# Layer 1's product with the eigenvector matrix as a burst on 64x64 blocks, and a second rank for the last units

## The chip, the cores and the metric

The kernel runs on one core of a Trainium2 chip. The time is the device time of one launch in microseconds, from the first to the last instruction of the program with what lies around it; less is better. Everything is fp32.

## The reference

Four graph layers follow each other on x, 128 graphs of 64 nodes with 256 features. Each is added to its input and normalised: `x = layernorm(x + layer(x))`.

- Layer 0: three times `(adj * adj) @ (h @ W)`, with relu after the first two; widths 512, 1024, 256.
- Layer 1: U holds the eigenvectors of a Laplacian of adj (found on the core itself). `agg = U.T @ x`, `h = relu(agg @ W1 + b1)` with 128 columns, `out = U @ (h @ W2 + b2)`.
- Layer 2: two graph convolutions with adj, then for p = 1 to 4 an LSTM over every window of p nodes (hidden size 256), whose last state replaces the window's last node.
- Layer 3: attention of each graph's nodes over each other, masked with adj.

## The kernel before, in words

The 8192 rows are cut into 16 groups of 512, that is 8 graphs. A tile of 128 rows holds two graphs, so a matrix over the nodes such as adj or U stands in a 128x128 tile with its 64x64 block twice on the diagonal (`adT2`, `adH2`, `u2`, `ut2`).

Until some 833 us layer 0 runs group by group, with the eigenvectors computed beside it. This stage is left as it was. From there on the 16 groups go through layers 1 to 3. Two groups form a unit, with its own instructions: `layer1` and `to_lstm` for each group (the latter with the steps for p = 1, `singles`, and p = 2, `pairs`), then `long` for p = 3 and p = 4 on both groups together, then `from_lstm` and `layer3` for each group. A step of an LSTM is `fast`: seven block products instead of eight for each gate, with sums and differences taken on DVE. Each step needs the state `hs` of the step before. The last unit is groups 14 and 15 (`ENDING`); its turns of data are done on PE, while the other groups' go through DVE transposes and a round trip through DRAM (`across`: one store and four loads on SP's queue). In `layer3` of the other groups there are two such round trips and eight small transfers of the attention weights.

In `layer1`, `mixed` applies U.T: 32 products on 64x64 blocks, four blocks of the array side by side, into two PSUM tiles that DVE and ACT copy out. Then comes the product with W1, bias and relu into `h`; then the turned product: with `h` as the held operand and `ut2` as the moving one, PE gives U applied to h, transposed, as `z`; then the product with W2. The turned product was made of 128x128 products, half of whose moving operand is zero, so four for each group.

The order of the instructions of all engines is written out by a planner, `Plan`. Every operation is noted with a cost and with what it depends on. `Plan.run` repeatedly picks the engine whose next operation can start first by its own clock, and on that engine, of the operations that can start within 0.02 us of the earliest, the one with the lowest `rank`. Up to four units (`UNITS`) are in progress; `todo` holds those that haven't begun. The rank is normally `op.due`, which is the group's number times `PERIOD` (17 us) less `op.tail`, the length of the chain of work that follows the operation. When nothing is left in `todo` and at most two groups (`LASTS`) are unfinished, PE prefers the group with more operations left. Buffers are slots by kind: eight PSUM tiles (`ps`), nine work tiles (`w`), four row tiles (`rows`) and so on. On the chip each engine then takes its instructions strictly in the order written, with semaphores for what comes from elsewhere; since they are emitted in one helper, nearly all of them have the line L162 in the profile.

Of the kernel before, what the change touches and what calls it, by code (L numbers as in the profile page):

```python
# [11 lines left out]
F32 = mybir.dt.float32  # L12
# [4 lines left out]
N = 64  # L17
# [86 lines left out]
class Plan:  # L104
# [59 lines left out]
    def run(self, units, ways):  # L164

        going, todo, held, left, wanted = {}, list(enumerate(units)), {}, {}, {}
        able = {e: [] for e in self.engines}

        def rank(op):
            if op.engine == "PE" and not todo and len(left) <= LASTS:  # L170
                return -left[op.group]
            return op.due

        def candidates(guard):
            oldest = min([u for u in going if u] or [0])
            best = None
            for e, ops in able.items():
                first = []
                for op in ops:
                    t = max(self.free[e], op.ready)  # L180
                    needs = {}
                    for tile in op.tiles:
                        if tile.real is None:
                            needs[tile.tag] = needs.get(tile.tag, 0) + 1
                    for tag, n in needs.items():
                        s = self.slots[tag]
                        t = max(t, sorted(s)[n - 1])

                        if (guard and op.unit != oldest and sum(x < 1e9 for x in s) < n +
                                min(self.MOST.get(tag, 1) - held.get((oldest, tag), 0), wanted.get((oldest, tag), 0))):  # L190
                            t = 1e9
                    if t < 1e9:
                        first.append((t, op))
                if first:
                    t0 = min(t for t, _ in first)
                    t, op = min((x for x in first if x[0] <= t0 + 0.02), key=lambda x: (rank(x[1]), x[1].rank))
                    if best is None or t < best[0]:
                        best = t, op
            return best

        while todo or going:
            while todo and len(going) < ways + (0 in going):
# [4 lines left out]
                for op in reversed(self.ops):  # L207
                    op.tail = op.cost + max([x.tail + (self.OWN if x.engine == op.engine else self.LAG)[op.engine]
                                             for x in op.after] or [0.0])
                    op.due = op.group * PERIOD - op.tail  # L210
                for tile in {tile: 0 for op in self.ops for tile in op.tiles if tile.real is None}:
# [5 lines left out]
            t, op = (candidates(True) if todo or len(left) > LASTS else None) or candidates(False)  # L217
            e = op.engine
            for tile in op.tiles:
                if tile.real is None:  # L220
                    s = self.slots[tile.tag]
# [533 lines left out]
P = 128  # L755
D = 256
# [8 lines left out]
OUTS = 2  # L765
LASTS = 2
PERIOD = 17.0
FARS = 8

RING = 4  # L770
QUADS = 1.17
# [58 lines left out]
def kernel(  # L830
# [25 lines left out]
    nc = tc.nc  # L856
    V, S, PE = nc.vector, nc.scalar, nc.tensor
# [5 lines left out]
    def tl(pool, shape, tag, **kw):  # L863
        uid[0] += 1
        return pool.tile(shape, F32, tag=tag, name=f"{tag}_{uid[0]}", **kw)
# [63 lines left out]
    ut2 = keep.tile([P, P], F32, name="ut2")  # L929
# [39 lines left out]
    def run(out, pairs):  # L969
        for i, (lhsT, rhs) in enumerate(pairs):  # L970
            mm(out, lhsT, rhs, i == 0, i == len(pairs) - 1)

    def relu(dst, src):
        S.activation(dst, src, AF.Relu)  # L974

    def quads(c):
        for m in (slice(0, N), slice(N, P)):
            for h, hs in enumerate((slice(0, N), slice(N, P))):
                yield m, slice(c * P + m.start, c * P + m.stop), h, hs
# [23 lines left out]
    spare = [lambda: tl(pa, [P, D], "spare")]  # L1003
    pending = []

    def step(then=None):

        while pending:
            pending.pop(0)()
        if then:  # L1010
            pending.append(then)
        if norms:
            norms.pop(0)()

    def bank(tag="ps"):
        return tl(psa, [P, 512], tag, bufs={"ps": 4, "ch": 2, "b5": 1}[tag])
# [40 lines left out]
    def seven(n, product, c11, c12, c21, c22, last):  # L1057

        def view(b):
            return b[:, :2 * n].rearrange("p (i n) -> p i n", i=2)  # L1060

        def add(dst, b):
            VL.tensor_add(dst, dst, b)
            if last is relu:
                relu(dst, dst)

        ch = view(bank("ch"))
        product(ch, 1, True)
        step(lambda: S.copy(c11, ch))
        yield  # L1070
        b2 = view(bank())
        product(b2, 2, True)
        step(lambda: add(c11, b2))
        yield
        product(ch, 6, False)
        step(lambda: S.copy(c12, ch))  # L1076
        yield
        b5 = view(bank("b5"))
        product(b5, 5, True)
        step(lambda: S.copy(c22, b5))  # L1080
        yield
        product(ch, 7, False)
        step(lambda: add(c22, ch))
        yield
        product(b5, 3, False)
        step(lambda: add(c12, b5))
        yield
        product(ch, 4, False)
        step(lambda: last(c21, ch))
        yield  # L1090
# [111 lines left out]
    wb = ctx.enter_context(tc.tile_pool(name="wb", bufs=1, reuse_waits="tile"))  # L1202
# [20 lines left out]

    far = [aside.tile([P, 1024], F32, name=f"far{i}") for i in range(FARS)]

    def place(tag, slot, shape):
# [8 lines left out]
        if tag in ("w", "v", "gates", "c", "hs"):  # L1235
# [3 lines left out]
    plan = Plan({"PE": nc.tensor, "DVE": nc.vector, "ACT": nc.scalar, "POOL": nc.gpsimd, "SP": nc.sync}, place,  # L1239
                {"ps": 8, "w": WIDE, "v": NARROW, "gates": GATES, "c": CELLS, "hs": OUTS, "att": ATT, "far": FARS, "rows": RING, "mx": 4, "sm": 4, "st": 4, "mv": 4,  # L1240
                 "rs": 4, "nm": 4})
    V, S, G, Q = (Noted(plan, e) for e in ("DVE", "ACT", "POOL", "SP"))
# [33 lines left out]
    def products(calls, also=(), **kw):  # L1276

        size = lambda x: x.at.size if isinstance(x, Part) else int(np.prod(x.shape[1:]))
        cost = sum(max(0.001673 * size(c[2]) + 0.003, 0.223) for c in calls)
        plan.note("PE", [("matmul", (o, l, r), {"start": a, "stop": z, **kw}) for o, l, r, a, z in calls], cost,  # L1280
                  also=also)
# [8 lines left out]
    def work():  # L1290
        return plan.tile("w", [P, 1024])

    def work2():
        return plan.tile("v", [P, 512])

    def ps4(shape=(P, 512)):
        return plan.tile("ps", shape)

    def as3(t, a):
        return t.rearrange("p (a b) -> p a b", a=a)  # L1300

    def relu(dst, src):
        S.activation(dst, src, AF.Relu)

    def mixed(src, rhs):

        dst = as3(work(), 2)
        to = dst.rearrange("p c (t h n) -> p h c t n", h=2, n=N)
        ps = [ps4((P, 2, 4, N)) for _ in range(2)]
        plan.note("PE", [("matmul", (ps[h][m, c, t, :], src[hs, t, f], rhs[hs, hs]), {"start": True, "stop": True})  # L1310
                         for t in range(4) for c in range(2) for m, f, h, hs in quads(c)], QUADS)
        V.tensor_copy(to[:, 0], ps[0])
        S.copy(to[:, 1], ps[1])
        return dst
# [22 lines left out]
    def layer1(xs):  # L1337
        a = mixed(xs, u2)
        for t in range(0, 4, 2):
            V.tensor_add(xs[:, t:t + 2, :], xs[:, t:t + 2, :], ub2.unsqueeze(1).to_broadcast([P, 2, D]))  # L1340
        h = as3(work2(), 4)
        z = work2()
        pz = ps4((P, 4, P))
        for t in range(0, 4, 2):
            p = ps4((P, 2, P))
            for j in range(2):
                run(p[:, j, :], [(a[:, k, (t + j) * P:(t + j + 1) * P], bw1[:, k, :]) for k in range(2)])
            V.tensor_add(h[:, t:t + 2, :], p, wide["b_b1"].unsqueeze(1).to_broadcast([P, 2, P]))
            relu(h[:, t:t + 2, :], h[:, t:t + 2, :])
            products([(pz[:, i, :], h[:, i, :], ut2, True, True) for i in (t, t + 1)])  # L1350
        S.copy(as3(z, 4), pz)
        for t in range(0, 4, 2):
            p = ps4((P, 2, D))
            for j in range(2):
                run(p[:, j, :], [(z[:, (t + j) * P:(t + j + 1) * P], bw2)])
            V.tensor_add(xs[:, t:t + 2, :], p, xs[:, t:t + 2, :])
            norm(xs[:, t:t + 2, :], False, twice=True)
# [388 lines left out]
```

## Time and profile before

| what | us |
|---|---|
| three runs | 2305.53, 2307.65, 2307.74 |
| median | 2307.65 |
| the profiled execution, own time | 2305.56 |
| its span from the first to the last instruction | 2303.8 |
| PE busy in the span | 2250.2 |
| weight loads busy (PEld) | 1985.7 |
| DVE busy | 1730.2 |
| ACT busy | 1196.0 |
| first instruction of layer 1 on PE | 832.8 |
| last product on PE starts | 2292.2 |

A row of the profile names the line, the engine, the operation, the tiles it writes and reads (out<-in, buffer numbers left out) and how many there are. PE is the matmul, PEld the weight load that runs beside it, DVE and ACT are the vector and the scalar engine, SP issues transfers. Matmuls are pipelined, so their durations overlap: the distance from one start to the next is what a product costs. An fp32 product appears as two records. In square brackets stands how long an engine was idle and which work ended that.

### The profile page before, as it was taken

To read this page: it belongs to the slowest core of one execution; us is meant where nothing else is said; L and a number is where in the kernel's file an instruction comes from. 1 tells how busy PE (TensorE), PEld (TensorE's weight loads), DVE (VectorE), ACT (ScalarE), POOL (GpSimd) and SP (SyncE) were. 2 spreads that over 40 slices of the span, in tenths; PEclk is the share of its full clock that TensorE was granted. 3 is DMA by queue.
4 is the path that set the end of the run, shared out by engine and by line. 5 is a ranking of instruction groups with operands and counts; after the bars stand their busy time and mean duration, and the time that the engine had idled before them with its cause. 6 is when DMAs were issued, how large, how long until landed. Compare 5 with 4: busy or idle time off the path is not lost.

```text
span 2303.8 us, 51099 instructions
## 1 busy us (share of the span) xinstructions
PE 2250.2 (98%) x20132; PEld 1985.7 (86%) x20132; DVE 1730.2 (75%) x5704; ACT 1196.0 (52%) x2892; POOL 137.0 (6%) x315
## 2 busy tenths in 40 slices
PE   8999999999999989999999999999999999999996
PEld 6788888878888778999989999899899899998895
DVE  5887877777888878666857967867866876878764
ACT  3444444443444336655556655555555655655654
POOL 0000000000000010000100100100000000000001
PEclk9999999999999999999999999999999999999998
DMA  7000000000000040000201211221211211312300
GB/s 242 11 11 11 10 11 11 19 11 11 11 10 2 1 161 20 19 1 27 85 22 57 75 56 40 78 72 40 77 56 49 76 65 31 104 58 93 99 19 19
DMA packets 80113, 107.87 MB, mean 47 GB/s; under 512 B 23296, under 2 KB 64256, under 8 KB 79872
## 3 DMA queue, kind: packets, MB, share of 16 engines
q1 hardware_dynamic: 79520, 104.32, 14.1%
q8 instruction: 158, 2.59, 0.5%
q14 instruction: 83, 0.68, 0.1%
q10 hardware_dynamic: 352, 0.28, 0.0%
HBM read 57.64 MB, written 45.09 MB: 45 GB/s over the span
## 4 chain that ended last, share of the span: by engine, by line
PE 86%; DVE 9%; ACT 1%; DMA 1%; issue 1%; POOL 1%; SPq 1%; DVEq 0%; ACTq 0%; POOLq 0%
PE ps L162 53%; PE ch L965 14%; PE ps L965 9%; PE b L965 6%; PE ps L1030 2%; DVE w L162 1%; DVE X L162 1%; DVE gates L162 1%; DVE st L162 1%; POOL rs L162 1%; DMA w<-far 1%; ACT gates L162 1%; PE pa L312 1%; SPq L162 1%; DVE D L52 1%
## 5 line engine op out<-in xcount | busy, mean ns | idle before, releaser
L162 PE MATMUL ps<-w,wih 128*128 128x128 f32 (+2 forms) x2944 | 573.0, 298 | 5.1 <-DVE gates L162 4.2
L162 PEld LDWEIGHTS ps<-w,wih 128*128 128x128 f32 x2944 | 454.3, 191 | 40.0 <-issue 13.5
L162 PE MATMUL ps<-w,sums 128*128 128x128 f32 (+2 forms) x3104 | 476.8, 294 | 5.7 <-DVE w L162 5.1
L162 PEld LDWEIGHTS ps<-w,sums 128*128 128x128 f32 x3104 | 419.9, 191 | 23.4 <-DVE w L162 6.4
L162 ACT ACTIVATE gates<-gates,cbi 128x256 f32<-128x256 f32 (+4 forms) x736 | 314.5, 479 | 189.0 <-DVE gates L162 186.0
L162 DVE TENSOR_TENSOR gates<-gates,ps 128x512 f32<-128x512 f32 (+4 forms) x408 | 235.9, 583 | 191.6 <-PE ps L162 182.4
L162 ACT COPY gates<-ps 128x512 f32<-128x512 f32 (+4 forms) x408 | 205.0, 507 | 238.1 <-PE ps L162 232.7
L162 PE MATMUL ps<-hs,whh 128*128 128x128 f32 (+1 forms) x896 | 182.2, 285 | 2.3 <-DVE hs L162 2.3
L162 PE MATMUL ps<-w,whh 128*128 128x128 f32 (+1 forms) x896 | 181.1, 284 | 0.0
L162 PEld LDWEIGHTS ps<-hs,whh 128*128 128x128 f32 x896 | 140.6, 193 | 2.5 <-DVE hs L162 2.5
L162 ACT ACTIVATE gates<-ps,cbi 128x128 f32<-128x128 f32 (+2 forms) x368 | 119.3, 385 | 42.2 <-PE ps L162 41.0
L162 PEld LDWEIGHTS ps<-w,whh 128*128 128x128 f32 x896 | 139.7, 191 | 0.0
L974 ACT ACTIVATE h<-h 128x512 f32<-128x512 f32 x96 | 60.5, 630 | 150.2 <-DVE h L52 150.2
L965 PE MATMUL ch<-m,tw 128*128 128x256 f32 x512 | 124.9, 382 | 3.0 <-ACT h L1076 1.7
L965 PE MATMUL b<-ss,aw 128*128 128x256 f32 x512 | 121.9, 379 | 0.0
L965 PE MATMUL ps<-aw,m 128*128 128x512 f32 x256 | 116.2, 606 | 1.2 <-ACT m L1036 1.2
L965 PEld LDWEIGHTS ch<-m,tw 128*128 128x128 f32 x512 | 94.7, 190 | 19.1 <-DVE h L52 3.7
L965 PEld LDWEIGHTS b<-ss,aw 128*128 128x128 f32 x512 | 96.8, 190 | 12.9
L162 POOL TENSOR_SCALAR rs<-mv 128x2 f32<-128x2 f32 x96 | 25.3, 272 | 1353.1 <-DVE mv L162 1351.7
L965 PEld LDWEIGHTS ps<-aw,m 128*128 128x128 f32 x256 | 48.3, 194 | 55.5 <-issue 51.5
L162 PE MATMUL ps<-hs,sums 128*128 128x128 f32 (+1 forms) x448 | 90.6, 284 | 0.0
L1036 ACT COPY m<-ps 128x512 f32<-128x512 f32 x96 | 51.2, 587 | 75.5 <-PE ps L1030 75.0
(360 smaller groups left out, 4077.4 us busy)
## 6 DMA issues: line engine op xcount, KB each, us to landing
far<-w SPq DMA_DIRECT2D x42, 512.0 KB, 2.7
w<-far SPq DMA_DIRECT2D x168, 128.0 KB, 3.2
X<-rest SPq DMA_DIRECT2D x24, 512.0 KB, 3.4
out_dram<-X SPq DMA_DIRECT2D x64, 128.0 KB, 1.7
rest<-XA SPq DMA_DIRECT2D x12, 512.0 KB, 2.6
rest<-X SPq DMA_DIRECT2D x12, 512.0 KB, 2.7
XA<-in_x_dram SPq DMA_DIRECT2D x22, 256.0 KB, 6.0
aw<-in_a_w_dram SPq DMA_DIRECT2D x3, 1024.0 KB, 10.2
```

Source lines behind the costliest of these rows:

```text
L52: return getattr(self.engine, name)(out, *args, **kw)
L162: getattr(e, name)(*[real(x) for x in args], **{k: real(v) for k, v in kw.items()})
L312: PE.matmul(out, lhsT, rhs, start=True, stop=True)
L965: PE.matmul(out, lhsT, rhs, start=start, stop=stop, **kw)
L974: S.activation(dst, src, AF.Relu)
L1030: PE.matmul(p[h][m, k, t, :], src[hs, t, f], sqT2[hs, hs], start=True, stop=True)
L1036: S.copy(to[:, h, c:c + 2], p[h])
```

## The change

Two things are changed in the program. In `layer1` the four turned products become one burst of 16 products on the four 64x64 blocks of the array; the halves of the result go to two PSUM tiles, of which DVE copies one and ACT the other. In `Plan.run` the rank of an operation is `op.due` only as long as some unit hasn't begun; from then on it is the group's number times `LATE` (8 us) less the tail. Also, the program is made with a smaller scratch for transfers that are described at run time (`dynamic_dma_scratch_size=1024`), and some helper functions are added that nothing calls.

```diff
         def rank(op):
             if op.engine == "PE" and not todo and len(left) <= LASTS:
                 return -left[op.group]
-            return op.due
+            return op.due if todo else op.group * LATE - op.tail
...
 PERIOD = 17.0
+LATE = 8.0
...
         h = as3(work2(), 4)
         z = work2()
-        pz = ps4((P, 4, P))
         for t in range(0, 4, 2):
             p = ps4((P, 2, P))
             for j in range(2):
                 run(p[:, j, :], [(a[:, k, (t + j) * P:(t + j + 1) * P], bw1[:, k, :]) for k in range(2)])
             V.tensor_add(h[:, t:t + 2, :], p, wide["b_b1"].unsqueeze(1).to_broadcast([P, 2, P]))
             relu(h[:, t:t + 2, :], h[:, t:t + 2, :])
-            products([(pz[:, i, :], h[:, i, :], ut2, True, True) for i in (t, t + 1)])
-        S.copy(as3(z, 4), pz)
+        pz = [ps4((P, 4, N)) for _ in range(2)]
+        plan.note("PE", [("matmul", (pz[b][m, i, :], h[bs, i, m], ut2[bs, bs]), {"start": True, "stop": True})
+                         for i in range(4) for m, _, b, bs in quads(0)], QUADS / 4 + 0.2)
+        to = z.rearrange("p (t h n) -> p h t n", h=2, n=N)
+        V.tensor_copy(to[:, 0], pz[0])
+        S.copy(to[:, 1], pz[1])
...
-    nc = bacc.Bacc("TRN2", target_bir_lowering=False, num_devices=1)
+    nc = bacc.Bacc("TRN2", target_bir_lowering=False, num_devices=1, dynamic_dma_scratch_size=1024)
```

More of the change, by code (lines that the diff above doesn't have):

```diff
@@ L1303, in relu, with two_by_two, sums_of, sums_moving @@
         S.activation(dst, src, AF.Relu)
+    def two_by_two(w):
+        return [[w[:, k, j * P:(j + 1) * P] for j in range(2)] for k in range(2)]
+    sevens = {}
+    def sums_of(key, w, stationary, ready, n=3):
+        s = plan.tile("sums", [P, n, P], wb.tile([P, n, P], F32, name=f"sums_{key}"))
+        (w00, w01), (w10, w11) = two_by_two(plan.tile("sums", [P, 2, D], w))
+        t1, t2, t4 = (s[:, i] for i in range(3))
+        t3 = s[:, 3] if n == 4 else w01
+        if stationary:
+            V.tensor_add(t1, w01, w11, ready=ready)
+            V.tensor_sub(t2, t1, w00, ready=ready)
+            V.tensor_sub(t4, w10, t2, ready=ready)
+            V.tensor_sub(t3, w00, w01, ready=ready)
+            sevens[key] = [None, w00, w10, t4, w11, t1, t2, t3]
+        else:
+            V.tensor_sub(t1, w01, w00, ready=ready)
+            V.tensor_sub(t2, w11, t1, ready=ready)
+            V.tensor_sub(t4, w10, t2, ready=ready)
+            V.tensor_sub(t3, w11, w01, ready=ready)
+            sevens[key] = [None, w00, w10, w11, t4, t1, t2, t3]
+    def sums_moving(b, spare):
+        (b00, b01), (b10, b11) = b
+        t1, t2 = spare
+        V.tensor_sub(t1, b01, b00)
+        V.tensor_sub(t2, b11, t1)
+        V.tensor_sub(b01, b11, b01)
+        return [None, b00, b10, b11, b10, t1, t2, b01], lambda: V.tensor_sub(b10, b10, t2)
+    def sums_held(a, spare):
+        (a11, a21), (a12, a22) = a
+        t1, t2 = spare
+        V.tensor_add(t1, a21, a22)
+        V.tensor_sub(t2, t1, a11)
+        V.tensor_sub(a21, a11, a21)
+        return [None, a11, a12, a12, a22, t1, t2, a21], lambda: V.tensor_sub(a12, a12, t2)
+    def seven(product, late, take, add):
+        chain, bank2, bank5 = (ps4((P, 2, P)) for _ in range(3))
+        def give(bank, i, new, also=()):
+            products(product(bank, i, new), also, skip_group_check=True)
+        give(chain, 1, True, (bank2,))
+        take(0, 0, chain)
+        give(bank2, 2, True)
+        add(0, 0, bank2)
+        late()
+        give(chain, 6, False)
+        take(0, 1, chain)
+        give(bank5, 5, True)
+        take(1, 1, bank5)
+        give(chain, 7, False)
+        add(1, 1, chain)
+        give(bank5, 3, False)
+        add(0, 1, bank5)
+        give(chain, 4, False)
+        take(1, 0, chain)
     def mixed(src, rhs):
```

## The prediction

> **What bounds the kernel now.** I read the page's busy shares first, then busy times by 30 us windows, then PE's timeline, then single waits. Each fp32 product leaves two records, so 16 groups x 4 turned products are 128 records.
>
> ```profile
> PE 2250.2 (98%) x20132; PEld 1985.7 (86%) x20132; DVE 1730.2 (75%) x5704; ACT 1196.0 (52%) x2892; POOL 137.0 (6%) x315
> ```
>
> ```profile
> 1980.00:2010.00 30.00, 30.00 (x324) 29.28 (x324) 28.90 (x88) 18.09 (x45) 3.88 (x8) 1.00 0.29 83
> 2190.00:2220.00 30.00, 30.00 (x219) 29.08 (x218) 21.17 (x65) 16.90 (x44) 1.99 (x4) 1.00 0.04 12
> 2220.00:2250.00 30.00, 25.94 (x215) 25.41 (x214) 17.29 (x50) 12.29 (x34) 1.94 (x4) 0.95 0.07 24
> 2250.00:2280.00 30.00, 22.72 (x159) 20.14 (x159) 14.15 (x43) 16.60 (x41) 4.82 (x16) 0.88 0.01 1
> 2280.00:2310.00 30.00, 11.49 (x97) 8.66 (x95) 13.22 (x50) 9.69 (x23) 5.10 (x16) 0.82 0.11 36
> ```
>
> Columns after the window: its length, then busy PE, PEld, DVE, ACT, POOL, the clock, DMA. PE is the bound: in the window at 1980 it never pauses, although DVE is busy 28.9 of 30 us. Only from 2220 on does it idle. So a PE saving before that is worth its full length, and the end can only be filled.
>
> What PE pays for a turned product and for a burst, from its timeline:
>
> ```profile
> 840.61 0.61 PE L162 MATMUL ps<-ut,v 128*128 128x128 f32 x4
> 841.06 0.61 PE L162 MATMUL ps<-bw,w 128*128 128x128 f32 x4
> 841.50 0.61 PE L162 MATMUL ps<-ut,v 128*128 128x128 f32 x4
> 842.04 1.16 PE L162 MATMUL ps<-u,X 64*64 64x64 f32 x64
> 843.13 0.48 PE L162 MATMUL ps<-bw,v 128*128 128x256 f32 x1
> ...
> 929.42 1.16 PE L162 MATMUL ps<-adH,X 64*64 64x64 f32 x64
> 930.41 1.11 PE L162 MATMUL ps<-adT,w 64*64 64x64 f32 x64
> 931.45 0.82 PE L162 MATMUL ps<-w,wih 128*128 128x128 f32 x5
> ```
>
> Starts count, not durations. Four full records take 841.06 - 840.61 = 0.45 us, 0.112 each. The last of the four at 841.50 starts at about 841.84, the burst at 842.04: entering costs 0.20 instead of 0.112, so 0.09 extra. One burst lasts 1.09 to the next full record, two in a row 931.45 - 929.42 = 2.03: 64 further records cost 0.94, 0.0147 each.
>
> And the waits:
>
> ```profile
> 1458.72 0.69 DVE L162 TENSOR_TENSOR X<-w,X 128x512 f32<-128x512 f32 x1 [2.28 <-DMA w<-far]
> 1460.59 1.12 PE L162 MATMUL ps<-w,sums 128*128 128x168 f32 x6 [1.91 <-DVE w L162]
> 2228.34 0.49 PE L162 MATMUL ps<-w,wih 128*128 128x128 f32 x2 [1.80 <-DVE gates L162]
> 2245.65 0.49 PE L162 MATMUL ps<-hs,whh 128*128 128x128 f32 x2 [2.27 <-DVE hs L162]
> 2247.18 0.63 PE L162 MATMUL ps<-hs,whh 128*128 128x128 f32 x2
> ```
>
> At 2228 and 2245 the last unit (groups 14, 15) is alone in its p = 4 steps and PE waits for its own recurrence. After the second wait a pair of records takes 0.43 us instead of 0.22 until 2250.5: eight pairs, 1.6 us more. At 1458 a DVE addition at the head of its queue waits for a transfer, and PE runs dry 1.9 us later; the chain of waits has such a transfer ahead of PE at 1641 and 1820 too.
>
> **What the Trainium skill says.** "TensorEngine Tiling (Array Packing)", Key Properties: another tiling mode drains the array first. The 0.09 us on entry agrees. "TensorE: Matmul & The Clock Gate", Part 3, The mechanism: products on different blocks overlap and start some 4 ns apart. Here 64 records start within about 1 us, 16 ns each on average, against 112. The same page, Part 1: idle PE brings a half-rate clock; the 0.43 against 0.22 after 2.27 us of idling agrees. Under Architectural detail it calls DVE's queue strictly in order; the wait at 1458 fits.
>
> **The change, part by part.**
>
> *Burst.* Removed per group: 4 products, 8 records x 0.112 = 0.90 us. Added: 16 block products, 32 records, half a burst: 1.09 - 32 x 0.0147 = 0.62, with 0.09 of entry 0.71. Saved 0.18 (unrounded), x16 = **2.9 us**, all on PE's path. Bounds: if half a burst costs just half (0.55 + 0.09) 4.2 us; if it needs 0.8 in all, 1.6.
>
> ```profile
> L162 ACT COPY v<-ps 128x512 f32<-128x512 f32 x16 | 9.2, 575 | 2.9 <-PE ps L162 2.8
> L162 DVE TENSOR_TENSOR v<-ps,wide_b_b 128x256 f32<-128x256 f32 x32 | 13.1, 415 | 5.3 <-PE ps L162 5.3
> L162 ACT COPY gates<-ps 128x256 f32<-128x256 f32 x48 | 17.3, 370 | 7.2 <-PE ps L162 6.7
> ```
>
> The copy out was one of 0.575 on ACT; now two halves run beside each other, 0.37 on ACT and about 0.415 on DVE (nearest row). DVE gets 16 x 0.415 = 6.6 us over 1470 us, behind a PE that doesn't wait at 28.9 of 30 us: nothing while DVE isn't the bound, at most 6.6 if it were so everywhere. The burst waits for all four blocks of h, not two; in 13 of the 16 groups of before the four products are issued together anyway, so nothing is put behind a new wait there. It takes two of the eight PSUM buffers, but for some 1.2 us instead of 2.2 (839.6 to 841.8): nothing. The smaller DMA scratch concerns POOL's own transfers, and the page's issues name only SP and ACT: nothing. The new helper functions aren't called.
>
> *Order at the end.* The rank changes once the last unit has begun, at product 5045 of 6768. The order of the instructions (counts, no times) shows what moves. From the last unit's third p = 3 step to its last p = 4 product, its own products are the same in both programs: 56 with 168 columns and 189 with 128. Before, only 8 products of older groups lie between them; in the changed program 16 of 512 columns, 64 block products of scores and 12 of 256: the attention of groups 10 to 13. PE in this stage, at start-to-start 0.143, 0.112, 0.429, 0.216 a record: before 16.0 + 42.3 + 3.5 = 61.8 us; it took 2191.2 to 2259.8 = 68.6. So **6.8 us** of waits and low clock can be filled. After: 58.3 + 13.7 + 4 x 1.13 (scores, 2122.89 to 2124.02) + 5.2 = 81.7, since 20 us of PE work came from earlier, where PE was full and now ends earlier.
>
> DVE has 213 instructions in that stage instead of 115. With the mean durations of the groups the older units need 51 us (40 norm statistics 11.3, 20 normalisations at 0.405, 23 transposes 14.0, 12 additions of attention at 0.474, softmax and the rest 12), the last unit 36 (18 additions of products 10.7, 34 cell operations 14.7, 36 sums 10.5): 87 us. Consecutive ones overlap: two of 0.68 at 835.68 took 1.28, so 0.07 each, 213 x 0.07 = 15, which leaves 72. PE's 81.7 lies between: stalls there of 0 to 5.5 us. The rate, 78 instructions in 30 us, is below the 88 of the window at 1980, where PE didn't wait, but lasts 80 us. SP's queue carries these groups' transfers closer together, with the head-of-queue wait of 1.9 as the price of a late one. I take one such wait and 1.1 us of DVE: **3.0 us given back**, range 0 to 7.4.
>
> *The final section.* From the turns of the last unit's state to the end, some 41 us, both programs run the same chain, with 112 products before and 116 after. What is left of groups 12 and 13 (four products and their norms) now shares DVE with it: two or three instructions of 0.4 in the chain's way, **1.0 us**; bounds 0 and 4.
>
> Sum: -2.9 - 6.8 + 3.0 + 1.0 = -5.7. The profiled execution took 2305.56 (span 2303.8 and 1.8 around it), so 2299.9. It lies at the low end of the three runs (2305.53 to 2307.74, median 2307.65); I add half of the 2.1 between: **2301.0 us**.
>
> **Rivals.**
> - *DVE becomes the bound of the end.* Its 87 us hold PE for 5.5, and one transfer for 1.9: 7.4 back instead of 3.0. 2299.9 + 4.4 + 1.1 = 2305.4, no change that shows. For it: 213 instructions in one stretch. Against it: 1980 to 2010.
> - *Transfers at the head of DVE's and PE's queues: slower.* Four groups each need two round trips and the eight small transfers of their attention in 80 us, twelve landings. A late one costs 1.9 (PE at 1460). The gains less the final section are 8.7 us, so the fifth late landing makes the kernel slower, and the eighth passes 0.2%. Nine: 2305.56 - 8.7 + 17.1 + 1.1 = 2315. For it: at the 1440 to 1470 window's DMA share of 0.43 PE lost 1.9. Against it: from 2120 to 2170, with four groups' transfers under way, PE waited 0.25 to 0.5 at a time only.
> - *The burst doesn't save*: alone among full products it pays entry and exit for half the work, and at 0.9 us it is even. 2301 + 2.9 = 2303.9.
>
> **How the numbers follow.** Two runs of this kernel differ by up to 0.1%, and 0.2% (4.6 us) is about what a measurement can tell from none: the limits are 2303.0 and 2312.3. Forecast 0.50, DVE bound 0.25, transfers 0.15, no saving 0.10. Faster: most of the forecast (0.45) and the low parts of DVE bound and no saving (0.10) = 0.55. Slower: the transfers and a tail of the others, 0.17. The rest, 0.28, is no change. Low end: 4.2 from the burst, all 6.8 filled and nothing given back, -11, with 1.1 added: 2295.7; as the altered costs also shift the order before the end, 2 us more: 2293.5. High end: DVE bound with 4 in the final section and the same 2, plus part of the transfers: 2312.
>
> **What would show it.** Right: 512 records of 64 x 64 blocks with ut, each burst some 0.6 us; no PE wait above 1 us in the last unit's p = 4 steps, no low clock there, DVE above 90% for the last 80 us before the final section. Wrong: a burst of 0.8 or more; PE waits on DMA or on DVE sums between these steps that add up to over 7 us; a final section above 45 us; new waits between 890 and 2190.

## The result, and the profile after

The changed kernel takes **2288.57 us** (median of four runs, 2287.95 to 2289.84); the kernel before took 2306.59 beside it on the same chip. The ratio is 0.9923, with a 95% interval of 0.9905 to 0.994. So it is faster by 18 us where 5.7 were forecast, and the time lies 4.9 below the low end of the range. The profiled execution has a span of 2288.0 us, 15.8 shorter than before. It is the slowest of the four, so the traces show 2 us less than the medians.

The row of busy shares on the page, which again leads to PE:

```profile
PE 2243.1 (98%) x20516; PEld 1978.4 (86%) x20516; DVE 1737.2 (76%) x5720; ACT 1189.1 (52%) x2892; POOL 134.9 (6%) x315
```

There are 384 more PE records (128 full ones became 512 small ones), but 7.1 us less busy PE. DVE has the 16 new copies.

The stretches of the end (window, length, then busy PE, PEld, DVE, ACT, POOL, clock, DMA share, GB/s). The first begins with the last unit's third p = 3 step, the third ends with its last p = 4 product, and the fourth is the final section:

```profile
2161.40:2190.00 28.60, 28.60 (x208) 24.40 (x209) 23.32 (x63) 16.20 (x37) 1.91 (x4) 1.00 0.38 115
2190.00:2220.00 30.00, 29.16 (x261) 26.31 (x257) 29.93 (x98) 14.23 (x36) 4.23 (x8) 1.00 0.54 164
2220.00:2244.90 24.90, 24.90 (x215) 22.59 (x213) 19.01 (x57) 11.91 (x30) 3.67 (x8) 1.00 0.45 127
2244.90:2288.00 43.10, 26.23 (x178) 20.34 (x177) 30.74 (x108) 22.64 (x57) 11.82 (x36) 0.83 0.15 45
```

In the three windows of the stage PE is busy for 82.66 of 83.5 us at full clock, where before the window at 2220 had 25.94 of 30 and a clock of 0.95. DVE is busy 72.26 us in it (87%, where the prediction named over 90% as a sign of being right), and in the middle window 29.93 of 30; PE still loses only 0.84 us there. That one pause, and the wait for the transfer near 1459, in the timeline (start, duration, in brackets the idle time and what ended it):

```profile
2192.84 0.49 PE L162 MATMUL ps<-hs,whh 128*128 128x128 f32 x2 [0.82 <-DVE hs L162]
```

```profile
1457.77 0.69 DVE L162 TENSOR_TENSOR X<-w,X 128x512 f32<-128x512 f32 x1 [2.37 <-DMA w<-far]
...
1459.63 1.12 PE L162 MATMUL ps<-w,sums 128*128 128x168 f32 x6 [2.00 <-DVE w L162]
```

The second is the wait of before: the DVE addition at the head of its queue again stands for a transfer, and PE, which has run dry by then, stands for 2.00 us until DVE has caught up. Neither edit touched that.

A burst of the turned product and the record after it on PE, and DVE's copy out in the list of groups (count, then busy us and mean ns, then idle time before):

```profile
1468.83 0.69 PE L162 MATMUL ps<-ut,v 64*64 64x64 f32 x32
1469.45 0.70 PE L162 MATMUL ps<-w,sums 128*128 128x256 f32 x2
```

```profile
L162 DVE COPY v<-ps 128x256 f32<-128x256 f32 x16 | 6.6, 414 | 0.2 <-PE ps L162 0.2
```

The burst occupies PE for 0.62 us to the next start, and a copy takes 0.414, as priced.

**Where the 15.8 us lie.** I set the PE records of both traces beside each other, product by product. What a start-to-start distance has above the usual one of its kind (0.112, 0.143, 0.216 and 0.429 us for 128, 168, 256 and 512 columns) is counted as a wait, low clock included. "Stage" is the stage of the prediction. All experiments, told below, are in the table. The waits are those of one profiled execution of each kernel; for e12 it is the slowest of its twelve, 4.3 us above their median.

| kernel | median us | ratio [95%] | PE waits: until group 14 begins | from there to the stage | in the stage | after it, to the last product | last product to end |
|---|---|---|---|---|---|---|---|
| before | 2306.59 | 1 | 24.0 | 5.1 | 6.7 | 13.1 | 11.6 |
| **after** | 2288.57 | 0.9923 [0.9905, 0.994] | 22.1 | 1.9 | 1.4 | 13.9 | 8.3 |
| e1 burst only | 2298.41 | 0.997 [0.9958, 0.9982] | 19.7 | 4.2 | 6.7 | 13.1 | 11.6 |
| e2 rank only | 2299.17 | 0.9975 [0.9964, 0.9986] | 21.7 | 3.0 | 5.7 | 13.9 | 8.3 |
| e3 rank from six groups on | 2295.14 | 0.9956 [0.994, 0.9973] | 21.8 | 6.3 | 2.5 | 15.1 | 7.6 |
| e4 old rank for the last two | 2288.04 | 0.9927 [0.9912, 0.9942] | 19.7 | 2.0 | 1.4 | 13.9 | 8.3 |
| e5 rank for PE alone | 2314.53 | 1.0038 [1.0024, 1.0052] | 19.4 | 22.8 | 2.3 | 13.3 | 11.5 |
| e6 rank for the others alone | 2301.25 | 0.9983 [0.9976, 0.9991] | 19.1 | 6.2 | 5.3 | 14.5 | 11.5 |
| e7 LATE = 0 | 2347.38 | 1.0185 [1.017, 1.0201] | 19.6 | 21.4 | 8.1 | 36.8 | 15.3 |
| e8 LATE = 4 | 2303.91 | 0.9999 [0.999, 1.0008] | 20.5 | 8.8 | 4.8 | 15.0 | 10.7 |
| e9 full products, same order | 2302.15 | 0.9984 [0.9977, 0.9991] | 19.1 | 1.9 | 1.4 | 14.2 | 8.3 |
| e10 burst noted at 0.72 | 2296.23 | 0.9961 [0.9946, 0.9975] | 21.6 | 1.0 | 6.8 | 14.4 | 7.9 |
| e11 LATE = 6 | 2293.41 | 0.9945 [0.9928, 0.9961] | 21.9 | 2.8 | 0.3 | 15.9 | 10.7 |
| e12 LATE = 12 | 2303.31 | 0.9991 [0.9982, 1.0] | 24.4 | 12.7 | 0.7 | 15.6 | 11.6 |

From before to after: waits -1.9, -3.2, -5.3 and +0.8, the end -3.2; PE's own work -3.4 (the full turned products -14.3, the block products +9.7, and +1.2 for thirteen more changes from full products to blocks, 0.093 each); layer 0, which wasn't changed, ended 0.9 later in this profile. That makes -15.3 of the -15.8. The first column of waits is the least certain: up to product 5043, where the new rank sets in, e1, e3 to e8, e11, e12 and after have the same written order, and still differ by 5 us in it.

One of e9's twenty executions took 9187 us for a reason that the record doesn't show, and its ratio leaves it out.

### The profile page after: what moved, and what is told of

Its sections match the earlier page's. It is cut to its first block, busy times and chain, and to the rows that moved or that the text cites. A ratio compares the mean times of both kernels' runs of the same rounds, so it can differ in the third digit from the quotient of the medians.

```text
span 2288.0 us, 51919 instructions
## 1 busy us (share of the span) xinstructions
PE 2243.1 (98%) x20516; PEld 1978.4 (86%) x20516; DVE 1737.2 (76%) x5720; ACT 1189.1 (52%) x2892; POOL 134.9 (6%) x315
## 3 DMA queue, kind: packets, MB, share of 16 engines
q1 hardware_dynamic: 79520, 104.32, 14.2%
## 4 chain that ended last, share of the span: by engine, by line
PE 90%; DVE 7%; issue 1%; ACT 1%; SPq 1%; DMA 1%; POOL 0%; DVEq 0%; ACTq 0%; POOLq 0%
PE ps L162 57%; PE ch L966 14%; PE ps L966 10%; PE b L966 6%; PE ps L1031 2%; DVE w L162 1%; PE pa L312 1%; DVE X L162 1%; DVE D L52 1%; DVE tw L52 1%; SPq L162 1%; DVE st L162 0%; DMA w<-far 0%; ACT gates L162 0%; DVE v L162 0%
## 5 line engine op out<-in xcount | busy, mean ns | idle before, releaser
L966 PEld LDWEIGHTS ch<-m,tw 128*128 128x128 f32 x512 | 94.7, 190 | 19.1 <-DVE h L52 3.8
L162 ACT ACTIVATE gates<-c 128x256 f32<-128x256 f32 (+1 forms) x176 | 76.4, 434 | 27.6 <-DVE c L162 26.1
## 6 DMA issues: line engine op xcount, KB each, us to landing
aw<-in_a_w_dram SPq DMA_DIRECT2D x3, 1024.0 KB, 10.1
```

The lines of the kernel that those rows point to most:

```text
L162: getattr(e, name)(*[real(x) for x in args], **{k: real(v) for k, v in kw.items()})
L966: PE.matmul(out, lhsT, rhs, start=start, stop=stop, **kw)
```

## The experiments

The ratios come from each kernel's own runs of before (medians of 2304.88 to 2306.59). The smaller transfer scratch of the change is in every kernel but before and e2, and wasn't tried alone.

**e1: the burst with the old rank.**

```diff
-            return op.due if todo else op.group * LATE - op.tail
+            return op.due
```

> The burst with the old rank throughout. Theory 1 (two parts that add up: the burst saves its own PE time, the rank at the end the rest): 4 us under before, 2302.6, each burst 0.62 us, and the waits of the last unit's p = 4 steps at 1.8 and 2.3 us as before. Rival (the burst's lower planner cost already changes the order well, the waits before the last unit's steps go with it): 9 us under before, 2297.6, with some 5 us less PE wait between 890 and 2190.

2298.41 us: faster by 0.3%, 6.9 us, more than twice the 2.9 priced, and nearer to the rival's 9 than to the 4 of theory 1. From the stage on its waits are those of before to 0.1 us, so all of it lies ahead: 3.3 of PE work and 5.2 fewer waits, less 1.2 by which layer 0 ended later. Part of the waits is chance, as the two timelines of PE around 1460 show. In e1 the wait for the transfer was 1.24 us, in after 2.00. First e1, then after:

```profile
1460.02 1.50 PE L162 MATMUL ps<-bw,w 128*128 128x128 f32 x12
1461.36 3.72 PE L162 MATMUL ps<-w,sums 128*128 128x256 f32 x20
```

```profile
1460.59 2.52 PE L162 MATMUL ps<-bw,w 128*128 128x128 f32 x12
1462.90 1.06 PE L162 MATMUL ps<-w,sums 128*128 128x256 f32 x2
```

The same twelve records take 1.34 us in one and 2.31 in the other: after the longer wait most of them run at half rate.

**e2: the rank without the burst.**

```diff
-            return op.due
+            return op.due if todo else op.group * LATE - op.tail
...
+LATE = 8.0
```

> The second rank without the burst: the turned products stay four full ones for each group. Theory 1: 14 us under before, 2292.6; no PE wait of 1.8 or more in the last unit's p = 4 steps. Rival: 9 us under before, 2297.6, and the waits from 2120 to 2175 stay.

2299.17, 5.8 us faster: less than expected, and not where expected. The stage holds as much work of older groups as in the changed kernel (83.38 us of busy PE), and still waits 5.7 us. Its windows (whole stage, then its middle) and two waits of PE:

```profile
2166.20:2253.60 87.40, 83.38 (x677) 73.77 (x676) 76.96 (x231) 42.03 (x100) 13.50 (x24) 1.00 0.46 141
2190.00:2220.00 30.00, 27.93 (x251) 24.46 (x249) 29.86 (x98) 15.76 (x39) 7.05 (x12) 1.00 0.57 167
```

```profile
2197.12 1.16 PE L162 MATMUL ps<-w,wih 128*128 128x128 f32 x8 [1.31 <-DVE gates L162]
...
2221.80 1.10 PE L162 MATMUL ps<-w,att 128*128 128x256 f32 x4 [1.76 <-issue]
```

In the middle window DVE is as full as in the changed kernel, but PE lacks 2.1 us instead of 0.8. Having work in the stage isn't enough: in this order PE stands at products of the last unit that wait for DVE, and for 1.76 us at an attention product for which the profile names no cause. What e2 gained lies mostly before the stage (4.4 us of waits, in part in the uncertain first column) and in the end, 11.6 to 8.3. The two edits alone add up to -12.7; together they gave -18. The excess of about 5 is at the edge of what the intervals can tell; the stage's waits, 5.7 against 1.4, differ by nearly as much.

**e3: the new rank only when at most six groups are unfinished. e4: the old one again for the last two groups.**

```diff
-            return op.due if todo else op.group * LATE - op.tail
+            return op.due if todo or len(left) > 6 else op.group * LATE - op.tail
```

> As the changed kernel, but the second rank begins only when at most six groups are unfinished (product 5748 instead of 5043 of 6768). If the gain comes from filling the last unit's steps and the final section alone: the same as the changed kernel, 2288.6, within 1.5. If it needs the earlier part, where the 5 us of waits before the last unit's third p = 3 step went: 2293 to 2294.

```diff
-            return op.due if todo else op.group * LATE - op.tail
+            return op.due if todo or len(left) <= LASTS else op.group * LATE - op.tail
```

> As the changed kernel, but with the old rank again once at most two groups are unfinished. If the rank in the final section shortens what follows the last product (11.6 us before, 8.3 in the changed kernel): 3 us slower than the changed kernel, 2291.8. If that end is shorter only because of what was already done before it: 2288.6 within 1.

e3 takes 2295.14, some 7 us more than after: 4.4 more waits from group 14 to the stage. So what is done long before the stage counts; whether that is the rank itself or the other order that it gives, e3 alone can't tell (see e10). e4 turned out to be no experiment: its edit changes not one instruction, the program is the changed kernel's byte for byte. Among the last two groups both ranks give the same order, so the shorter end (8.3) is set before them. As a second profile of the same program it shows what chance alone does: 19.7 and 22.1 us of waits before group 14, and the same to 0.1 us from there on.

**e5 and e6: the new rank for PE alone, and for the other engines alone.**

```diff
-            return op.due if todo else op.group * LATE - op.tail
+            return op.due if todo or op.engine != "PE" else op.group * LATE - op.tail
```

> The burst, and the second rank for PE's operations alone; DVE, ACT, POOL and SP keep the old one. If the gain is the filling of PE's queue in the last unit's steps: within 2 us of the changed kernel, 2287 to 2291. If the last unit's own DVE and ACT operations must be put ahead too: 2294 or more, with PE waits on DVE in its p = 4 steps.

```diff
-            return op.due if todo else op.group * LATE - op.tail
+            return op.due if todo or op.engine == "PE" else op.group * LATE - op.tail
```

> The mirror of it: the second rank for DVE, ACT, POOL and SP, the old one for PE. If the gain is PE's filling: as the burst alone, 2298 to 2299, with the waits of 1.8 and 2.3 us in the last unit's steps. If the other queues matter: 2291 to 2295.

With PE alone the kernel is slower than before, 26 us above after. One wait makes up 9.8 of that. In e5 the wait on PE, and the window of the ten us ahead of it:

```profile
2167.09 3.14 PE L162 MATMUL ps<-w,sums 128*128 128x168 f32 x10 [9.82 <-DVE w L162]
```

```profile
2157.00:2167.00 10.00, 0.27 (x2) 0.00 (x0) 10.00 (x32) 0.96 (x3) 1.82 (x4) 0.66 0.51 179
```

PE stands for the sums of the last unit's products, and DVE is busy all the ten us, with older groups' attention, norms and transposes among what stands ahead of these sums in its queue. This lies before the stage, and not in the p = 4 steps as expected. With the others alone nothing comes out beyond the burst alone (2301.25 against 2298.41). In this kernel the rank paid only where all engines followed it.

**e7 and e8: LATE = 0 and LATE = 4**, which keep more of the older groups for the end (168 and 140 products after the last p = 4 product instead of 116).

```diff
-LATE = 8.0
+LATE = 0.0
```

> As the changed kernel with LATE = 0, so the length of the chain that follows decides alone. 168 products are left after the last unit's last p = 4 product instead of 116: more attention of groups 10 to 13 lies in the final section, where PE waited 13.7 us. If PE's waits are what counts: 3 to 5 us faster than the changed kernel, 2284 to 2286. If DVE bounds the end (the rival of the prediction): slower than it by 3 to 8 us, 2292 to 2297, as 52 more products' DVE work goes into the final chain.

```diff
-LATE = 8.0
+LATE = 4.0
```

> LATE = 4: 140 products after the last unit's last p = 4 product. Between the changed kernel and LATE = 0 if the effect is one of filling: 2286 to 2288 in the first case, 2290 to 2293 in the second.

LATE = 4 gives back the whole gain, LATE = 0 is 1.85% slower than before. Single waits on PE, in e7 and then in e8:

```profile
1945.44 1.19 PE L162 MATMUL ps<-w,att 128*128 128x256 f32 x2 [6.70 <-DMA att<-v]
...
2307.96 4.14 PE L162 MATMUL ps<-ident,X 128*128 128x128 f32 x16 [17.38 <-ACT X L162]
```

```profile
2266.69 1.97 PE L162 MATMUL ps<-ident,w 128*128 128x128 f32 x8 [8.16 <-DVE w L162]
```

The windows ahead of the last wait of each, again e7 and then e8, and the normalisation that e7 waits for:

```profile
2286.00:2308.00 22.00, 3.79 (x9) 2.56 (x9) 12.94 (x47) 0.69 (x2) 7.02 (x21) 0.50 0.37 126
2258.50:2266.70 8.20, 0.04 (x2) 0.01 (x1) 8.20 (x27) 1.62 (x4) 3.91 (x11) 0.60 0.23 70
```

```profile
2307.31 1.09 ACT L162 ACTIVATE X<-X,nm,rs 128x256 f32<-128x256 f32 x2 [36.27 <-POOL nm L162]
```

In e7 an attention product waits 6.7 us for its small transfers at the head of PE's queue. Its last wait is for no full engine: ACT had been idle for 36 us, and DVE was busy for 12.94 of 22. The chain of waits leads from ACT over POOL and DVE to a load (`X<-rest`, 4.5 us on its way) that SP issued after a row of stores. In e8 DVE was busy all the 8.2 us, with norms and attention of other groups. So e7 shows the slower rival of the prediction, transfers at the heads of queues, and e8 a crowded DVE: 59 us at LATE = 0 and 15 at LATE = 4 above the changed kernel, both far beyond what either expectation allowed.

**e9: the burst taken back, the order kept.** Eight full products of 64 columns in its place, noted at the same cost; every instruction else stands where it stands in the changed kernel.

```diff
-        plan.note("PE", [("matmul", (pz[b][m, i, :], h[bs, i, m], ut2[bs, bs]), {"start": True, "stop": True})
-                         for i in range(4) for m, _, b, bs in quads(0)], QUADS / 4 + 0.2)
+        plan.note("PE", [("matmul", (pz[b][:, i, :], h[:, i, :], ut2[:, b * N:(b + 1) * N]), {"start": True, "stop": True})
+                         for i in range(4) for b in range(2)], QUADS / 4 + 0.2)
```

> Same written order of every instruction as the changed kernel; only the burst is taken back: the 16 block products become 8 products with the whole 128x128 block of h held and one 64-column half of ut2 moving (half of each operand is zero again), into the same two PSUM tiles and with the same two copies. Theory 1 (the burst is worth only what it saves on PE, the remainder of its -7 in the burst-only kernel came from another order): the 16 records of a group cost 0.06 to 0.112 us each, 0.95 to 1.8 against 0.72 for the burst, so 2288.6 + 16 x (0.23 to 1.1) = 2292 to 2306, and the distance to the changed kernel is 16 times the distance between the two in the timeline, to 1 us, with the waits of every section unchanged. Theory 2 (the shorter hold of PSUM tiles or an earlier z also removes waits): the distance is 2 us or more above that product, and new PE waits stand after these products.

On PE, in e9, such a set and what follows it:

```profile
841.97 1.90 PE L162 MATMUL ps<-ut,v 128*128 128x64 f32 x16
843.80 1.16 PE L162 MATMUL ps<-u,X 64*64 64x64 f32 x64
```

Sixteen records take 1.75 us on the average of the 16 groups, 0.109 each: with half the columns a record costs as much as with 128. PE's work grows by 27.99 - 9.67 for the bursts - 1.49 for sixteen entries = 16.8 us, and the time by 14 (2302.15 against 2288.57; by the ratios 14.1, give or take 4). The waits from group 14 on are those of the changed kernel to 0.3 us; before that e9 has 3.0 less, which accounts for the rest and lies within the spread of that column. So with the order held, PE time in `layer1` reaches the end for the most part, and no hidden gain from the shorter hold of the PSUM tiles shows: theory 2 falls. Theory 1's "to 1 us" was too narrow for the chance in the early waits.

**e10: the burst noted at what it takes.** Same work, same rank; the planner counts 0.72 us instead of 0.4925.

```diff
-                         for i in range(4) for m, _, b, bs in quads(0)], QUADS / 4 + 0.2)
+                         for i in range(4) for m, _, b, bs in quads(0)], 0.72)
```

> The changed kernel with the burst entered in the planner at 0.72 us instead of 0.4925, which is what it takes on the chip; the work is the same, the written order differs from product 96 on. Theory 1 (the 5 us by which both edits together beat the sum of each alone are an accident of the written order): a kernel with the same work and another order lies somewhere else between 2288 and 2297, with waits of 1.4 to 6 us in the stage between the last unit's third p = 3 step and its last p = 4 product. Theory 2 (the gain belongs to the edits, whatever the order): within 1.5 us of 2288.6, with the waits of the stage at 1.4 to 2.0.

2296.23, 7.7 slower than the changed kernel by nothing but another order. Its stage waits 6.8 us, and a head-of-queue wait for a transfer is back on PE:

```profile
2185.02 1.96 PE L162 MATMUL ps<-w,dw 128*128 128x512 f32 x4 [2.36 <-DMA w<-far]
```

That is an older group's attention asking for its turned data, which a load of a round trip brings, 2.4 us late. Some 1.6 us of the stage's 6.8 are records at half rate after a pause of 1.31. Theory 1 holds, with a little more waiting than its 6 us: the order alone moves the time by several us.

**e11 and e12: LATE = 6 and LATE = 12.**

```diff
-LATE = 8.0
+LATE = 6.0
```

> LATE = 6 instead of 8. 120 products instead of 116 are left after the last p = 4 product. Theory 1 (there is a best distance between keeping older groups for the end and finishing them in time, flat around 8): 2289 to 2294, between the 2288.6 of LATE = 8 and the 2303.9 of LATE = 4, and what is lost stands as PE waits after the last unit's turns. Theory 2 (the curve is rough, since each value gives another written order): 2295 or more, or below 2288.

```diff
-LATE = 8.0
+LATE = 12.0
```

> LATE = 12 instead of 8: older groups are put ahead more, so less of their work is left for the last unit's p = 4 steps; again 116 products after the last of these. Theory 1 (flat around 8): 2288 to 2293, with the last unit starting later than in the changed kernel and more PE waits in its p = 4 steps (2 to 5 us). Theory 2 (rough): 2295 or more, with one or two PE waits above 2 us somewhere after 1975.

At 6 it is 2293.41: the stage is as full as it can be (0.3 us of waits), but the end is 2.4 longer and 2.0 more is waited ahead of it. That fits a best value between. At 12 it is 2303.31, which is beyond what a flat optimum allows: 12.7 us of waits from group 14 to the stage, none of them over 2 us, and some 3 of them records at half rate. So 4, 6, 8 and 12 give 2304, 2293, 2289 and 2303. That fits a narrow optimum near 8 as well as a rough curve; with one order for each value, and orders that differ by 7.7 us at the same value (e10), these runs can't tell which. No run was better than the changed kernel by more than its interval.

## Why the prediction fell short

- **What bounds the kernel.** Right. PE bounds it outside the end, and 16.8 us of added PE work cost 14 (e9).
- **The burst, -2.9.** Right in its mechanism and price: 0.62 was forecast with 0.09 for the entry, and 0.625 with 0.093 was measured for the thirteen bursts that a full product follows. It saved 3.4, 0.5 more than forecast: the other three stand directly ahead of another burst, take 0.515, and spare that one its entry. DVE's copy (0.414, forecast 0.415) costs nothing that shows: in the stage DVE's busiest 30 us cost PE 0.84. The half full-width products of e9 weren't an alternative, at 0.109 a record.
- **The stage, 6.8 to be filled and 3.0 given back.** The sums were right: 81.7 us of PE work and 72 of DVE were forecast, 82.66 and 72.26 measured. The amount given back was mis-sized: 1.4 us of waits are left instead of 3.0, a gain of 5.3 instead of 3.8. The point from which DVE decides wasn't reached. But the runs show that this term can't be had from the sums: with about the same filling the waits are 0.3, 1.4, 5.7 and 6.8 us in e11, after, e2 and e10. A range of 0 to 7.4 was right, and the value within it is set by the written order.
- **"20 us of PE work came from earlier, where PE was full": the first step that failed.** PE wasn't full there. From the first product of group 14 to the stage it waited 5.1 us before and 1.9 after, so 3.2 us came from a stretch that the prediction counted as nothing. The window at 1980 that was shown never pauses, but it is one window, and it was taken for the whole stretch. These are the last two of before ahead of the stage:

```profile
2130.00:2160.00 30.00, 29.10 (x190) 24.97 (x190) 26.37 (x79) 18.21 (x44) 4.12 (x8) 1.00 0.37 121
2160.00:2191.20 31.20, 30.04 (x244) 27.09 (x243) 22.27 (x61) 20.48 (x50) 0.00 (x0) 1.00 0.27 67
```

  The prediction had even met such pauses, of 0.25 to 0.5 us from 2120 to 2170, but used them only as an argument against a rival. The difference isn't one of where the count begins: before waits 0.3 us between product 5043 and its group 14. It isn't one lucky order either: e2, e10 and e11, with the rank for all engines in three other orders, wait 1.0 to 3.0 here, e1 with the old rank 4.2 and e3, in which the rank comes later, 6.3. But a LATE of 4 or 12 waits 8.8 and 12.7, and e5, in which only PE follows the rank, 22.8. What in the order spares the waits isn't shown. In the changed kernel group 14 begins its `layer1` at 1902 instead of 1977, so the last unit's own work is spread over more of the older groups; that alone isn't enough, as it begins as early in e5 (1901).
- **The final section, +1.0: the second step that failed, in sign.** It took 43.2 us instead of 44.2 and holds 1.7 us more of PE's work, four more products. Waits in it rose by 0.8, near the 1.0 forecast, but from the last product to the end it takes 8.3 us instead of 11.6. The timeline shows what follows the last products on PE. First before, then after:

```profile
2291.46 1.13 PE L162 MATMUL ps<-w,v 128*128 128x256 f32 x4 [0.52 <-ACT v L162]
2291.48 0.85 DVE L162 SCALAR_TENSOR_TENSOR X<-ps,sm,X 128x256 f32<-128x256 f32 x2
...
2292.91 0.86 DVE L162 SCALAR_TENSOR_TENSOR X<-ps,sm,X 128x256 f32<-128x256 f32 x2
...
2295.07 0.22 POOL L162 TENSOR_SCALAR rs<-mv 128x2 f32<-128x2 f32 x1 [4.04 <-DVE mv L162]
...
2299.10 2.07 ACT L162 ACTIVATE X<-X,nm,rs 128x256 f32<-128x256 f32 x4 [1.33 <-POOL nm L162]
```

```profile
2278.28 2.08 PE L162 MATMUL ps<-w,v 128*128 128x256 f32 x4 [0.52 <-ACT v L162]
...
2280.40 0.88 DVE L162 SCALAR_TENSOR_TENSOR X<-ps,sm,X 128x256 f32<-128x256 f32 x2 [1.79 <-PE ps L162]
...
2282.31 0.22 POOL L162 TENSOR_SCALAR rs<-mv 128x2 f32<-128x2 f32 x1 [2.03 <-DVE mv L162]
...
2283.94 1.09 ACT L162 ACTIVATE X<-X,nm,rs 128x256 f32<-128x256 f32 x2 [2.54 <-POOL nm L162]
```

  Before, DVE is behind: four attention additions and their statistics are still to be done when PE begins its last products, then POOL makes the roots of three pairs one after the other, and ACT's last six normalisations follow at 2296.68 and 2299.10. After, two additions are left, one round of POOL and two normalisations. The prediction counted the products of the final section and took the chain after them as given. The shorter end comes with the rank for all engines at LATE = 8: e2 has it without the burst, e3 and e10 in other orders (7.6 and 7.9), e5 and e6 haven't it. It isn't secured by the rank, though: with LATE = 6 it is 10.7, with 12 it is 11.6 again.
- **Elsewhere.** -1.9 in the waits before group 14 and +0.9 in layer 0 weren't forecast; both are within what kernels of the same order differ by.
- **The rivals.** DVE as the bound of the end: DVE was full for 30 us, but PE lost 0.84; it does become the bound where PE's order runs ahead of its own (e5). Transfers at the heads of the queues: none holds PE in the last part of the changed kernel, but e7 and e10 show them, with 6.70 and 2.36 us at a time instead of the 1.9 used as the price. The burst doesn't save: fell with the records.
- **Small slips.** The rank sets in at product 5043, not 5045; 2295.7 less 2 is 2293.7, not 2293.5; and near 1460 PE doesn't run dry 1.9 us after DVE's wait, its pause of 1.9 us ends there. None of them matters for the result.

By the sum: burst -0.5, stage -1.5, the stretch before it -3.2, the final section -3.4, the rest -1.0 against the forecast, 9.6 of the 10.1 that the traces differ by. Of the two thirds that lie in the stretch before the stage and in the end, the range had nothing: its "2 us more" for a shifted order was too little, where the same work in other orders spreads by 7.7 us (e10).

What stays open is why this order has so few waits and that of e2 or e10 more. Which of the planner's picks decides it wasn't tried. That the changed kernel has the best of the orders tried, and lies 7.7 us below e10, is in part luck of the order.

## What to carry to other kernels

Where a change alters the order in which a planner or scheduler writes instructions, count the gain by stretches over everything after the first moved instruction, up to the last one on any engine, and not only over the stage it is meant for; a window without a pause speaks for itself alone. Give such a change a range at least as wide as the same work spreads when the order shifts (here some 8 us, found by noting one operation at another cost), and let all engines follow the same preference: with PE alone following it, this kernel was 26 us slower. And where idle time can be filled, filling more isn't better: from LATE = 8 to 4 the gain was gone.

## What the runs showed of the hardware

- A short pause can halve PE's rate, and needn't. In all the kernels PE pauses near 1460 us (e9 at 1467) and waits for DVE. Of the seven waits of 1.83 to 2.00 us there, five were followed by records at half rate, some 1.5 us lost (before, after, e3, e11, e12), and two were not (e5, e8); of the seven of 1.16 to 1.62 us none was. Beside the 2.00 us of after, shown above, stands e5:

```profile
1460.49 1.12 PE L162 MATMUL ps<-w,sums 128*128 128x168 f32 x6 [1.99 <-DVE w L162]
1461.45 1.50 PE L162 MATMUL ps<-bw,w 128*128 128x128 f32 x12
1462.79 3.72 PE L162 MATMUL ps<-w,sums 128*128 128x256 f32 x20
```

  The same twelve records take 1.34 us here. Likewise the wait of 2.27 us in the last unit's p = 4 steps, which the prediction read: e6 has it with 2.26 us, and runs on at full rate after it. The Trainium skill, "TensorE: Matmul & The Clock Gate", Part 1, HAM oscillation, warns of idle gaps above about 3.4 us; here little more than half of that was enough in some runs, so to a wait of 2 us for a transfer up to 1.5 more may have to be added. In e10 pauses of 1.31 and 0.48 us within 2 us were followed by half rate, in e2 the same pair, at 2197, was not.
- A full fp32 product with 64 columns costs 0.109 us a record, with 128 columns 0.112 (e9). Here halving the columns alone saved nothing, while the burst on the blocks, at 0.6 us for 32 records, did.
- DVE can be busy 29.93 of 30 us beside a PE that pauses for 0.84 us. In e2 DVE's 29.86 went with 2.1 us that PE lacked, so the share alone doesn't tell the stalls.
